# A LayerNorm, attention and ternary FFN kernel: both ends reordered, and two half-filled stationaries packed into one

## The chip, the cores and the metric

The kernel runs on one core of a Trainium2 chip. Its time is device microseconds from start to end of one execution; the figure for a kernel is the median of its runs. A core has a tensor engine (TensorE, in the profile PE, with weight loads as PEld), a vector engine (DVE), a scalar engine (ACT), GpSimd (POOL) and a synchronisation engine (SP). Each takes its instructions strictly in order and waits on semaphores for the others. DMAs are issued from the instruction streams of SP and ACT (in the profile SPq and ACTq). In this kernel TensorE multiplies a stationary of at most 128x128 by a moving operand of at most 512 columns and writes to PSUM, from which DVE and ACT read.

## The reference

The input x is 2048 x 256 (one batch, 32-bit floats). One layer normalisation feeds two branches, and both are added to x:

```python
xn = layernorm(x)                      # no scale, no offset
qkv = xn @ Wqkv.T                      # 16 heads of 128 for q, k and v
w = softmax(q @ k.T * 128 ** -0.5)     # 2048 x 2048 per head, no mask
attention = (w @ v) @ Wout.T           # 2048 -> 256
x1 = xn @ quantize(w1).T               # 256 -> 704
x2 = xn @ quantize(w2).T               # 256 -> 704
ffn = (sigmoid(x1) * x2) @ quantize(w3).T   # 704 -> 256
out = x + attention + ffn

def quantize(w):                       # weights -1, 0, 1
    gamma = mean(abs(w))
    return clip(round(w / (gamma + 1e-8)), -1, 1)
```

The inner width of the FFN, 704, is five times 128 and a rest of 64.

## The kernel before

**Sizes.** Rows are worked on in four chunks of 512 (NB = 4, QB = 512), each of four tiles of 128 (TB = 4). The key dimension has 16 tiles (NKT). Heads come in pairs (G = 2) whose weights are loaded together. The FFN's inner width has six chunks f (FC = 6); the last has only 64 columns. All orders are written out by hand: each engine does its instructions in the order in which the program makes them.

**The front (lines 320 to 344).** `loads` issues all early loads. Then one turn for each row chunk c: `turned` transposes the normalised chunk on PE (eight transposes, line 215, tile `pxn`), ACT copies it to `xnT` (line 216); `normalized` makes the next chunk on DVE; `magnitude` lets ACT sum the absolute values of one FFN matrix (tile `abs`); `q_piece(0, c)` and `v_piece(0, 2 * c)` make q of head 0 and one of eight v pieces of the first pair; `magnitude_of_all` sums over partitions by a matmul with ones (tile `pg`). After the four turns `quantize` makes the three ternary matrices on DVE (`w0q`, `w1q`, `w2q`: one comparison into `low`, one into the result), and `k_piece(0, c)` makes k of head 0. `halved` splits a value into a high part (ACT cast to the f32r type) and a low part (DVE): products with exact ternary weights are made from both parts.

**The FFN loop (lines 345 to 354).** 24 steps (c, f). `hidden` makes both first products of a step, w1's into one bank of a PSUM tile `ph` and w2's into the other: four matmuls each (line 275; 64 stationary columns where f is 5). ACT takes the sigmoid, DVE multiplies, `halved` splits. `summed` runs two steps later and adds the step's part of the second product into two PSUM tiles `pf` (line 297); after f = 5 ACT copies them to `yT`. `added` transposes `yT` back (line 314, tile `pyt`) and DVE adds it to y (line 317). The last `summed` and `added` run inside the attention's first steps.

**PSUM and small banks.** There are three two-bank tiles of the tag s (scores, `ph`, `pxn`, `pyt`), one bank m and one bank av. Before the attention's steady part, `bank` deals m and av out in turn to q, k and v pieces; ACT's copy of a piece frees its bank.

**Attention (lines 453 to 522).** Block n is one head and one row chunk, 64 in all; step v is one row tile, 256 in all. `scores(v)` makes two score tiles (line 374), DVE takes maxima (line 379), ACT exponentials (line 388). `exchanged(v)` moves the 128 x 2048 block of exponentials between partition groups by 16 DMAs of 64 KB, ten from SP and six from ACT (line 398); `transposed(v)` finishes the transposition on DVE in 32x32 squares (line 415) into `pT`. `weighted(n, k)` multiplies v by `pT` (line 421, tile `av`), ACT copies the result to `oT` (line 428), `projected(n, u)` multiplies by the output weights (line 439, tile `po`), and DVE scales by the inverse sums and adds into y (line 445). Scores run six steps ahead (LEAD) of `weighted`; in these first six steps, fillers from the table `first` stand between scores:

```python
1: [("v", 0, 1), ("v", 0, 3)], 2: [("v", 0, 5), ("v", 0, 7)],
3: [("k", 1, 0), ("k", 1, 1)], 4: [("k", 1, 2), ("q", 1, 0)], 5: [("k", 1, 3), ("q", 1, 1)],
```

In the steady part, k and q pieces of the next head and one v piece of the next pair per block are spread over the steps. A row chunk's result goes out by one DMA of 512 KB (line 450).

Of the kernel before, what the change touches and what calls it, by code (L numbers as in the profile page):

```python
# [19 lines left out]
def layernorm_attention_bitffn_kernel(  # L20
# [14 lines left out]
    nc = tc.nc  # L35
# [110 lines left out]
    def loads(fraw):  # L146
# [17 lines left out]
        for i, (src, cols) in enumerate(((w1T, FF), (w2T, FF))):  # L164
            w = fraw.tile([P, KC, FF], F32, tag=f"w{i}", name=f"w{i}s")
            nc.sync.dma_start(w, src.rearrange("(c p) f -> p c f", p=P))
            raw.append(w)
# [3 lines left out]
        if rest:  # L171
            nc.gpsimd.memset(w[:, whole, :], 0.0)
# [3 lines left out]
        if rest:  # L176
            nc.sync.dma_start(w[:rest, whole, :], w3T[whole * P :, :])
# [39 lines left out]

    ones = fw.tile([P, P], F32, tag="ones", name="ones")
# [16 lines left out]
    def quantize(fraw, i: int, w):  # L235

        wf = w.rearrange("p c f -> p (c f)")

        pos = fraw.tile([P, 1], F32, tag=f"pos{i}", name=f"pos{i}")
        neg = fraw.tile([P, 1], F32, tag=f"neg{i}", name=f"neg{i}")  # L240
        nc.vector.tensor_scalar(
            pos, pgs[0][:, 0, i : i + 1], 0.5 / (FF * DM), 0.5 * Q_EPS, ALU.mult, ALU.add
        )
        nc.vector.tensor_scalar(neg, pos, -1.0, None, ALU.mult)
        low = fraw.tile([P, FC * DM], F32, tag="low", name=f"low{i}")
        lo = low[:, : wf.shape[1]]
        wq = fw.tile(list(w.shape), F32R, tag=f"w{i}q", name=f"w{i}q")
        nc.vector.tensor_scalar(lo, wf, neg, None, ALU.is_lt)
        nc.vector.scalar_tensor_tensor(
            wq.rearrange("p c f -> p (c f)"), wf, pos, lo, ALU.is_gt, ALU.subtract  # L250
        )
        quantized[i] = wq
# [3 lines left out]

    xs, hids, yTs = {}, {}, {}

# [10 lines left out]
    def hidden(fp, c: int, f: int):  # L269
        m = min(P, FF - f * P)  # L270
        ph = ps_s.tile([P, 2, QB], F32, tag="s", name=f"ph{c}_{f}")
        todo = [(d, i) for i in (1, 0) for d in range(KC)]
        for j in range(2):
            for d, i in todo:
                nc.tensor.matmul(  # L275
                    ph[:m, j, :], quantized[j][:, d, f * P : f * P + m], xs[c][i][:, d],
                    start=((d, i) == todo[0]), stop=((d, i) == todo[-1]),
                )
        sg = fp.tile([P, QB], F32, tag="sg", name=f"sg{c}_{f}", bufs=2)
        nc.scalar.activation(sg[:m], ph[:m, 0, :], AF.Sigmoid)  # L280
        nc.vector.tensor_tensor(sg[:m], sg[:m], ph[:m, 1, :], ALU.mult)
        hid = [fp.tile([P, QB], F32R, tag=f"hid{i}", name=f"hid{i}{c}_{f}", bufs=4) for i in "hl"]
        halved(hid[0][:m], hid[1][:m], sg[:m])
        hids[c, f] = hid

    def summed(fp, c: int, f: int):

        m = min(P, FF - f * P)
# [6 lines left out]
        for e in range(DM // P):  # L295
            for i in (1, 0):
                nc.tensor.matmul(  # L297
                    yTs[c][e], quantized[2][:m, f, bass.ts(e, P)], hid[i][:m],
# [8 lines left out]
    def added(c: int):  # L307

        yT = yTs.pop(c)
        pt = ps_s.tile([P, 2, QB], F32, tag="s", name=f"pyt{c}")  # L310
        ptv = pt.rearrange("p a (b e) -> p (a b) e", e=DM)
        for t in range(TB):
            for e in range(DM // P):
                nc.tensor.transpose(  # L314
                    ptv[:, t, bass.ts(e, P)], yT[:, e, bass.ts(t, P)], ident
                )
        nc.vector.tensor_tensor(ys[c], ptv, ys[c], ALU.add)  # L317


    with tc.manual_schedule():  # L320
# [5 lines left out]
        with tc.tile_pool(name="fraw", bufs=1) as fraw:  # L326
            raw = loads(fraw)
            xns = {0: normalized(fraw, 0)}
            for c in range(NB):
                turned(xns.pop(c), c)  # L330
                if c + 1 < NB:
                    xns[c + 1] = normalized(fraw, c + 1)
                if c:
                    magnitude(fraw, c - 1, raw[c - 1])
                q_piece(0, c)
# [3 lines left out]
            for i, w in enumerate(raw):  # L339
                quantize(fraw, i, w)  # L340
                if i == 0:
                    halved_x(0)
        for c in range(NB):
# [3 lines left out]
        for i, (c, f) in enumerate(chunks):  # L347
# [3 lines left out]
            if i > 1:  # L351
# [65 lines left out]
    def weighted(n: int, k: int):  # L417
        h, b = blocks[n]
        if k == 0:
            avs[n] = ps_av.tile([P, QB], F32, tag="av", name=f"av{n}")  # L420
        nc.tensor.matmul(  # L421
            avs[n], vs[h // G, k // 2][:, k % 2, bass.ts(h % G, D)],
            pTs[n].rearrange("p t g (k q) -> p (t g) k q", q=32)[:, :, k, :],
            start=(k == 0), stop=(k == NKT - 1),
        )
        if k == NKT - 1:
            oT = apool.tile([P, QB], F32, tag="oT", name=f"oT{n}", bufs=1)
            nc.scalar.copy(oT, avs.pop(n))  # L428
            oTs[n] = oT

    def projected(n: int, u: int):

        h, b = blocks[n]
        if n == NBK - 1 and u % 2:
            pm = ps_s.tile([P, 2, QB], F32, tag="s", name=f"po{n}_{u}")[:, :, :DM]
        else:
            pm = ps_m.tile([P, 2, DM], F32, tag="m", name=f"po{n}_{u}")
        for j in range(2):
            nc.tensor.matmul(  # L439
                pm[:, j, :], oTs[n][:, bass.ts(2 * u + j, P)], weights[h // G, "o"][:, h % G, :],  # L440
# [8 lines left out]
        if u == TB // 2 - 1 and h == H - 1:  # L449
            nc.sync.dma_start(  # L450
                out[b * QB : (b + 1) * QB, :].rearrange("(t p) d -> p t d", p=P), ys[b]
            )
# [5 lines left out]
        1: [("v", 0, 1), ("v", 0, 3)], 2: [("v", 0, 5), ("v", 0, 7)],  # L458
        3: [("k", 1, 0), ("k", 1, 1)], 4: [("k", 1, 2), ("q", 1, 0)], 5: [("k", 1, 3), ("q", 1, 1)],
# [3 lines left out]
    with tc.manual_schedule():  # L463

        nc.scalar.activation(warm, ident[:, 0:1], AF.Exp)
        for u in range(-LEAD, NBK * TB):
# [7 lines left out]
            if lead_in:  # L474
# [9 lines left out]
                elif v == 3 and H > G:  # L484
                    load_weights(1, "v")
            elif t == 0:
                if n // GB + 1 < H // G:
                    v_piece(n // GB + 1, n % GB)
# [30 lines left out]
        inverses(NBK - 1)  # L519
        for u in range(TB // 2):  # L520
            projected(NBK - 1, u)
# [38 lines left out]
```

## Time and profile before

| What | us |
|---|---|
| median of three runs | 2309.71 (2309.66 to 2311.34) |
| profiled execution, its own time | 2309.66 |
| its span, first to last instruction | 2307.9 |
| PE busy | 2286.2 |
| DVE busy | 1463.5 |
| ACT busy | 771.8 |
| idle of PE that waits name | 16.3 |
| granted TensorE clock, mean | 0.998 |

In the page and the views, a group's name is line, engine, operation and tiles, written as out<-in with buffer numbers left out. A wait row reads: engine and line, what released it, us in total, times, longest. A busy PE is not PE at its peak: matmuls are pipelined, so that the start-to-start time of a run of matmuls says more than the length of one. A timeline row gives start, length, engine, line, operation, tiles, count, and in brackets the idle time before it and what ended it.

### The profile page before, as it was taken

How to read it: one execution, taken by the hardware profiler on the slowest of the kernel's cores; microseconds unless marked ns; L12 is line 12 of the kernel's file. 1: busy time of each engine (PE TensorE's matmuls, PEld its weight loads, DVE VectorE, ACT ScalarE, POOL GpSimd, SP SyncE). 2: the span in 40 equal slices, each digit the busy share in tenths (PEclk: the TensorE clock that was granted, in tenths of full speed). 3: DMA queues.
4: the chain of work that ended last, by engine and by line, in shares of the span. 5: the costliest groups of instructions: out<-in, count | busy, mean ns of one | idle time of the engine just before them, and what ended most of it. 6: DMA issues, size and time to landing. Idle time of an engine off the chain costs nothing.

```text
span 2307.9 us, 22750 instructions
## 1 busy us (share of the span) xinstructions
PE 2286.2 (99%) x6022; PEld 1136.2 (49%) x6022; DVE 1463.5 (63%) x1800; ACT 771.8 (33%) x1360; POOL 1.1 (0%) x8
## 2 busy tenths in 40 slices
PE   8999999999999999999999999999999999999997
PEld 6754444444444444444444444444444444444443
DVE  6566666666666666666666666566566666666774
ACT  5443333333333333323333333333333333333331
POOL 0000000000000000000000000000000000000000
PEclk9999999999999999999999999999999999999999
DMA  2055555555554555555555555555545555555554
GB/s 93 0 144 136 132 122 129 124 136 121 127 127 119 137 127 120 125 131 133 119 123 131 130 125 126 125 123 137 127 119 126 126 136 122 121 128 128 136 140 107
DMA packets 210977, 284.89 MB, mean 123 GB/s; under 512 B 66272, under 2 KB 79264, under 8 KB 210848
## 3 DMA queue, kind: packets, MB, share of 16 engines
q1 hardware_dynamic: 136448, 182.03, 32.6%
q10 hardware_dynamic: 74400, 101.42, 18.3%
q8 instruction: 47, 0.77, 0.2%
q14 instruction: 82, 0.67, 0.1%
HBM read 12.65 MB, written 2.10 MB: 6 GB/s over the span
## 4 chain that ended last, share of the span: by engine, by line
PE 97%; SPq 1%; DMA 0%; ACT 0%; DVE 0%; issue 0%; ACTq 0%; DVEq 0%
PE s L374 38%; PE av L421 37%; PE pq L116 5%; PE pv L132 5%; PE pk L106 5%; PE po L439 5%; PE ph L275 2%; PE pf L297 1%; SPq L398 1%; DMA part<-p 0%; PE pxn L215 0%; ACT xnT L216 0%; ACT p L388 0%; PE pyt L314 0%; DMA y<-in_x_dram 0%
## 5 line engine op out<-in xcount | busy, mean ns | idle before, releaser
L379 DVE TENSOR_REDUCE mx<-s 128x1 f32<-128x1024 f32 x512 | 627.0, 1225 | 706.8 <-PE s L374 706.8
L388 ACT ACTIVATE p<-s,nm 128x1024 f32<-128x1024 f32 x512 | 566.1, 1110 | 1394.8 <-DVE nm L382 627.1
L421 PE MATMUL av<-pT,v 128*128 128x512 f32 x2048 | 922.1, 593 | 6.3 <-DVE ri L405 6.3
L374 PE MATMUL s<-kT,qT 128*128 128x512 f32 x2048 | 921.1, 592 | 1.4 <-DVE y L317 1.3
L415 DVE STREAM_TRANSPOSE pT<-part 128x1024 f32<-128x1024 f32 x512 | 606.4, 1223 | 22.3 <-DMA part<-p 11.2
L374 PEld LDWEIGHTS s<-kT,qT 128*128 128x128 f32 x2048 | 388.9, 190 | 464.4 <-issue 440.2
L421 PEld LDWEIGHTS av<-pT,v 128*128 128x128 f32 x2048 | 389.7, 190 | 445.9 <-issue 439.6
L445 DVE SCALAR_TENSOR_TENSOR y<-po,ri,y 128x256 f32<-128x256 f32 x256 | 112.0, 479 | 31.8 <-PE po L439 17.2
L439 PE MATMUL po<-wo,oT 128*128 128x256 f32 x512 | 131.3, 379 | 0.7 <-ACT oT L428 0.7
L439 PEld LDWEIGHTS po<-wo,oT 128*128 128x128 f32 x512 | 97.2, 190 | 68.5 <-issue 60.3
L116 PE MATMUL pq<-xnT,wq 128*128 128x512 f32 x256 | 120.7, 594 | 4.4 <-ACT xnT L216 4.4
L132 PE MATMUL pv<-wv,xnT 128*128 128x256 f32 x512 | 120.6, 379 | 0.0
L106 PE MATMUL pk<-xnT,wk 128*128 128x512 f32 x256 | 119.7, 592 | 0.0
L132 PEld LDWEIGHTS pv<-wv,xnT 128*128 128x128 f32 x512 | 97.3, 190 | 39.7 <-issue 29.2
L388 ACT ACTIVATION_READ_ACCUMULATOR p<-s,nm 128x1 f32 x512 | 100.3, 196 | 0.0
L116 PEld LDWEIGHTS pq<-xnT,wq 128*128 128x128 f32 x256 | 48.3, 190 | 64.7 <-issue 59.3
L106 PEld LDWEIGHTS pk<-xnT,wk 128*128 128x128 f32 x256 | 48.6, 190 | 60.7 <-issue 60.7
L428 ACT COPY oT<-av 128x512 f32<-128x512 f32 x64 | 37.5, 586 | 75.5 <-PE av L421 75.5
L382 DVE TENSOR_REDUCE nm<-mx 128x1 f32<-128x2 f32 x256 | 39.7, 155 | 28.2 <-DVE mx L379 1.4
L121 ACT ACTIVATE qT<-pq 128x512 f32<-128x512 f32 x64 | 38.1, 595 | 1.8 <-PE pq L116 1.8
L137 ACT COPY v<-pv 128x512 f32<-128x512 f32 x64 | 37.1, 583 | 4.5 <-PE pv L132 4.5
L110 ACT COPY kT<-pk 128x512 f32<-128x512 f32 x64 | 37.2, 583 | 3.8 <-PE pk L106 3.8
(67 smaller groups left out, 330.6 us busy)
## 6 DMA issues: line engine op xcount, KB each, us to landing
part<-p SPq DMA_DIRECT2D x2560, 64.0 KB, 2.0
part<-p ACTq DMA_DIRECT2D x1536, 64.0 KB, 2.1
wq<-in_wqkvT_dram SPq DMA_DIRECT2D x8, 256.0 KB, 2.9
wv<-in_wqkvT_dram SPq DMA_DIRECT2D x8, 256.0 KB, 2.9
wk<-in_wqkvT_dram SPq DMA_DIRECT2D x8, 256.0 KB, 2.9
wo<-in_woutT_dram SPq DMA_DIRECT2D x8, 256.0 KB, 2.8
out_dram<-y SPq DMA_DIRECT2D x4, 512.0 KB, 3.0
y<-in_x_dram SPq DMA_DIRECT2D x2, 512.0 KB, 7.9
```

What stands on the lines that cost most here:

```text
L106: nc.tensor.matmul(pm, w[:, d, bass.ts(h % G, D)], xnT_k[:, d, c], start=(d == 0), stop=(d == KC - 1),)
L116: nc.tensor.matmul(pm, w[:, d, bass.ts(h % G, D)], xnT[:, d, bass.ts(c, QB)], start=(d == 0), stop=(d == KC - 1),)
L132: nc.tensor.matmul(pm[:, j, :], xnT[:, d, bass.ts(2 * i + j, P)], w[:, d, :], start=(d == 0), stop=(d == KC - 1),)
L275: nc.tensor.matmul(ph[:m, j, :], quantized[j][:, d, f * P : f * P + m], xs[c][i][:, d], start=((d, i) == todo[0]), stop=((d, i) == todo[-1]),)
L374: nc.tensor.matmul(s[:, bass.ts(j, QB)], qTs[h, b][:, bass.ts(t, P)], kTs[h][:, i * HALF + j * QB : i * HALF + (j + 1) * QB], start=True, ...
L379: nc.vector.tensor_reduce(mx[:, i : i + 1], s, AX.X, ALU.max)
L382: nc.vector.tensor_reduce(nm, mx, AX.X, ALU.max, negate=True)
L388: nc.scalar.activation(p, s, AF.Exp, bias=nm, accum_out=sums[n][:, t, i : i + 1],)
L415: nc.vector.transpose(pTs[n][:, t, g : g + 2], part[:, g : g + 2])
L421: nc.tensor.matmul(avs[n], vs[h // G, k // 2][:, k % 2, bass.ts(h % G, D)], pTs[n].rearrange("p t g (k q) -> p (t g) k q", q=32)[:, :, k, ...
L439: nc.tensor.matmul(pm[:, j, :], oTs[n][:, bass.ts(2 * u + j, P)], weights[h // G, "o"][:, h % G, :], start=True, stop=True,)
L445: nc.vector.scalar_tensor_tensor(ys[b][:, t, :], pm[:, j, :], rinvs[n][:, t : t + 1], ys[b][:, t, :], ALU.mult, ALU.add,)
```

## The change

- Front: `quantize` of the first two matrices moves into the turns 2 and 3. Turns 1, 2 and 3 get one more v piece (1, 3, 5), ahead of the q piece. `halved_x(0)` stands ahead of the last `quantize`. Two of the four k pieces of head 0 move between the first steps of the FFN loop.
- Last FFN chunk: the last 64 columns of both first matrices are quantized into one stationary `wlast` of 128 columns. `hidden` makes one product for f = 5: the first matrix's results lie on partitions 0 to 63, the second's on 64 to 127. ACT's sigmoid goes from the lower to the upper partitions, and all that follows, the last rows of w3 too, stands on partitions 64 to 127.
- Hand-over: the last `added` uses two tiles from `bank`, of four transposes each, and not a tile s; DVE adds in two halves. The table `first` holds the last v piece, head 1's pieces, and three v pieces of the second pair, which blocks 0 to 2 no longer make; the second pair's v weights are loaded at step 1, not 3.
- Tail: the last block's `weighted` and `projected` leave the loop. The columns of block 63 are made in two halves, the second in a tile s, with the projections of block 62 and of the first half between them. The last head's results go out by two tiles in a DMA, those of the last block by one tile, the last of each pair from ACT.

```diff
-            nc.gpsimd.memset(w[:, whole, :], 0.0)
+            nc.gpsimd.memset(w[:LAST, whole, :], 0.0)
...
-            nc.sync.dma_start(w[:rest, whole, :], w3T[whole * P :, :])
+            nc.sync.dma_start(w[LAST:, whole, :], w3T[whole * P :, :])
...
+    LAST = P - FF % P
...
-        wq = fw.tile(list(w.shape), F32R, tag=f"w{i}q", name=f"w{i}q")
...
-        nc.vector.scalar_tensor_tensor(
-            wq.rearrange("p c f -> p (c f)"), wf, pos, lo, ALU.is_gt, ALU.subtract
-        )
+        lo = lo.rearrange("p (c f) -> p c f", c=w.shape[1])
+        if i == 0:
+            quantized["last"] = fw.tile([P, KC, P], F32R, tag="wlast", name="wlast")
+        whole = FF // P * P if i < 2 else w.shape[2]
+        wq = fw.tile([P, w.shape[1], whole], F32R, tag=f"w{i}q", name=f"w{i}q")
+        parts = [(wq, 0, whole)]
+        if i < 2:
+            parts.append((quantized["last"][:, :, i * LAST : (i + 1) * LAST], whole, FF))
+        for o, f0, f1 in parts:
+            nc.vector.scalar_tensor_tensor(
+                o, w[:, :, f0:f1], pos, lo[:, :, f0:f1], ALU.is_gt, ALU.subtract
+            )
...
     def hidden(fp, c: int, f: int):
-        m = min(P, FF - f * P)
...
-        for j in range(2):
+        if f == FC - 1:
+            ws = [quantized["last"]]
+        else:
+            ws = [quantized[j][:, :, bass.ts(f, P)] for j in range(2)]
+        for j, w in enumerate(ws):
             for d, i in todo:
                 nc.tensor.matmul(
-                    ph[:m, j, :], quantized[j][:, d, f * P : f * P + m], xs[c][i][:, d],
+                    ph[:, j, :], w[:, d], xs[c][i][:, d],
...
+        p0 = LAST if f == FC - 1 else 0
...
-        nc.scalar.activation(sg[:m], ph[:m, 0, :], AF.Sigmoid)
-        nc.vector.tensor_tensor(sg[:m], sg[:m], ph[:m, 1, :], ALU.mult)
+        nc.scalar.activation(sg[p0:], ph[: P - p0, 0, :], AF.Sigmoid)
+        nc.vector.tensor_tensor(sg[p0:], sg[p0:], ph[p0:, len(ws) - 1, :], ALU.mult)
...
-                    yTs[c][e], quantized[2][:m, f, bass.ts(e, P)], hid[i][:m],
+                    yTs[c][e], quantized[2][p0:, f, bass.ts(e, P)], hid[i][p0:],
...
     def added(c: int):
...
+        if c < NB - 1:
+            pt = ps_s.tile([P, 2, QB], F32, tag="s", name=f"pyt{c}")
+            pts = [pt.rearrange("p a (b e) -> p (a b) e", e=DM)]
+        else:
+            pts = [bank([P, 2, DM], f"pyt{c}_{u}") for u in range(2)]
...
+            y = ys[c][:, u * m : (u + 1) * m]
+            nc.vector.tensor_tensor(y, pt, y, ALU.add)
...
+                if c > 1:
+                    quantize(fraw, c - 2, raw[c - 2])
                 if c:
                     magnitude(fraw, c - 1, raw[c - 1])
+                if c:
+                    v_piece(0, 2 * c - 1)
                 q_piece(0, c)
...
-            for i, w in enumerate(raw):
-                quantize(fraw, i, w)
-                if i == 0:
-                    halved_x(0)
-        for c in range(NB):
+            halved_x(0)
+            quantize(fraw, len(raw) - 1, raw[-1])
+        for c in range(2):
             k_piece(0, c)
...
-            if i > 1:
+            if i < 2:
+                k_piece(0, i + 2)
+            else:
                 summed(fp, *chunks[i - 2])
...
-    def weighted(n: int, k: int):
+    def weighted(n: int, k: int, part=None):
+
         h, b = blocks[n]
+        t0, t1 = (0, TB) if part is None else (part * TB // 2, (part + 1) * TB // 2)
         if k == 0:
-            avs[n] = ps_av.tile([P, QB], F32, tag="av", name=f"av{n}")
+            pool, tag = (ps_s, "s") if part else (ps_av, "av")
+            avs[n] = pool.tile([P, QB], F32, tag=tag, name=f"av{n}_{t0}")
...
-        if u == TB // 2 - 1 and h == H - 1:
-            nc.sync.dma_start(
-                out[b * QB : (b + 1) * QB, :].rearrange("(t p) d -> p t d", p=P), ys[b]
-            )
+
+            if h == H - 1 and (j or n == NBK - 1):
+                t0 = t if n == NBK - 1 else t - 1
+                (nc.scalar if n == NBK - 1 and j else nc.sync).dma_start(
...
-        1: [("v", 0, 1), ("v", 0, 3)], 2: [("v", 0, 5), ("v", 0, 7)],
-        3: [("k", 1, 0), ("k", 1, 1)], 4: [("k", 1, 2), ("q", 1, 0)], 5: [("k", 1, 3), ("q", 1, 1)],
+        1: [("v", 0, NV - 1), ("k", 1, 0)], 2: [("k", 1, 1), ("k", 1, 2)],
+        3: [("k", 1, 3), ("q", 1, 0)], 4: [("q", 1, 1), ("v", 1, 0)], 5: [("v", 1, 1), ("v", 1, 2)],
...
-        for u in range(-LEAD, NBK * TB):
+        for u in range(-LEAD, (NBK - 1) * TB):
...
-                elif v == 3 and H > G:
                     load_weights(1, "v")
             elif t == 0:
-                if n // GB + 1 < H // G:
-                    v_piece(n // GB + 1, n % GB)
+                g = n // GB + 1
+                if g < H // G and ("v", g, n % GB) not in made:
+                    v_piece(g, n % GB)
...
-        inverses(NBK - 1)
-        for u in range(TB // 2):
-            projected(NBK - 1, u)
+
+        n = NBK - 1
+        for i in range(n - 1, n + 1):
+            inverses(i)
+        for k in range(NKT):
+            weighted(n, k, 0)
+            if k in (KQ - 1, 3 * KQ - 1):
+                projected(n - 1, k // (2 * KQ))
+        for k in range(NKT):
+            weighted(n, k, 1)
+            if k == KQ - 1:
+                projected(n, 0)
+        projected(n, 1)
```

## The prediction

> **What bounds the kernel now.** First the page's busy shares: TensorE (PE) has work 99% of the span, and its chain row gives PE 97%. So the end moves by what PE no longer does, and by the holes in its work. The list of PE's waits names every hole:
>
> ```profile
> PE 2286.2 (99%) x6022; PEld 1136.2 (49%) x6022; DVE 1463.5 (63%) x1800; ACT 771.8 (33%) x1360; POOL 1.1 (0%) x8
> ```
> ```profile
> PE av L421 <- DVE ri L405: 6.3, 1, 6.3
> PE pq L116 <- ACT xnT L216: 4.4, 4, 1.1
> PE pf L297 <- issue: 2.2, 1, 2.2
> ...
> PE s L374 <- DVE y L317: 1.3, 1, 1.3
> PE po L439 <- ACT oT L428: 0.7, 1, 0.7
> ```
>
> All lie within 126 us of the start or 32 us of the end; between, PE issues without a hole. The stage windows (columns: stretch; its length, then busy us and count by engine; PEclk is the granted clock) show what two holes cost besides: after 2.2 and 6.3 us idle the clock is granted at 0.63 and 0.71, near half for some 3.5 us.
>
> ```profile
> 47.40:51.60 4.20, 4.20 (x14) 3.34 (x13) 3.24 (x5) 2.66 (x4) 0.00 (x0) 0.63 0.00 0
> ...
> 126.00:2276.30 2150.30, 2150.30 (x5488) 1042.34 (x5486) 1384.17 (x1644) 708.16 (x1261) 0.00 (x0) 1.00 0.54 129
> 2276.30:2287.90 11.60, 5.32 (x9) 2.27 (x9) 2.59 (x4) 0.59 (x1) 0.00 (x0) 0.71 0.27 77
> ```
>
> Two more timelines (start, length, engine, line) carry the sum: ScalarE (ACT) at the hand-over from FFN to attention, where its copies of v stand behind two exponentials and six DMA issues; and the last 32 us.
>
> ```profile
> 119.77 5.00 ACTq L398 DMA_DIRECT2D part<-p  x5
> 124.87 1.11 ACT L388 ACTIVATE p<-s,nm 128x1024 f32<-128x1024 f32 x1 [4.80 <-DMA part<-p]
> ...
> 127.06 0.58 ACT L137 COPY v<-pv 128x512 f32<-128x512 f32 x1
> ...
> 127.53 0.60 ACT L137 COPY v<-pv 128x512 f32<-128x512 f32 x1
> ```
> ```profile
> 2276.45 0.59 ACT L428 COPY oT<-av 128x512 f32<-128x512 f32 x1 [7.59 <-PE av L421]
> ...
> 2280.18 2.37 DVE L415 STREAM_TRANSPOSE pT<-part 128x1024 f32<-128x1024 f32 x2 [3.98 <-DMA part<-p]
> ...
> 2282.69 5.41 PE L421 MATMUL av<-pT,v 128*128 128x512 f32 x8 [6.28 <-DVE ri L405]
> ...
> 2300.86 1.99 PE L439 MATMUL po<-wo,oT 128*128 128x256 f32 x8 [0.73 <-ACT oT L428]
> 2302.03 1.74 DVE L445 SCALAR_TENSOR_TENSOR y<-po,ri,y 128x256 f32<-128x256 f32 x4 [7.57 <-PE po L439]
> ```
>
> Start-to-start prices, from the timeline: a 512-column f32 matmul is two instructions of 0.43 us, a 256-column one two of 0.215; an FFN product (f32r) is one of 0.23. So a q, k or v piece is 1.72 us and 32 `av` instructions are 13.7. Below, times are on the old trace's clock.
>
> **The front (0 to 51.6 us): 7.2 us gained.** Three v pieces (3 x 1.72 = 5.16 us) move from later work, which PE bounds, into the turns of the chunk loop, where PE waits 1.1 us for each `xnT` copy. Turn 1: transposes start at 13.95 and take 0.87; v1 to 16.57; q1 to 18.29. v2 needs the bank that v1's copy frees, and that copy stands on ACT behind `abs0` (17.98 + 0.19), so it ends near 18.7: a wait of 0.45. v2 to 20.46, `pg` to 20.75. Turns 2 and 3 are 0.87 + 3 x 1.72 + 0.3 = 6.3 each without a wait, by the same copying on ACT: 33.4, where the old kernel was at 31.49.
>
> VectorE (DVE): the first two quantizations (3.2 us each, with 0.15 to 0.3 for each added small piece) move into its idle stretches; `xl0`, behind v6's copy and the cast, is ready at 36.2, and the third quantization ends at 39.4. PE does k0, k1 to 36.9, so it doesn't wait for `xl0`. With k2, k3 between the first hidden chunks, hidden, k, hidden, k, hidden end at 45.8. The old first `pf` started 4.2 after the end of `w2q` (42.05 to 46.24); by the same chain it could start at 43.6, so the 2.2 us wait is gone, and with it the half-clock stretch. The next `pf`, hidden, `pf` take 3.65 and end at 49.5; the old kernel got there at 51.57. Gain 2.07 + 5.16 = 7.2. Bounds: 5 (a bank wait like 0.45 in every turn, a late `pf`) to 7.7 (no wait at all).
>
> **Last FFN chunk: 3.7 us gained.** The eight 64-column products of a chunk lasted 54.29 to 56.13, as long as eight of 128 columns. Four go, four times: 16 x 0.23 = 3.7. What follows them on ACT and DVE keeps its count and length (64 partitions took 0.59 and 0.68 against 0.60 and 0.69), and `summed` still comes two chunks later: 3.7 us (1.83 + 0.91 + 0.92) beside a chain of 3.0. Products from the upper 64 rows stand in no row; those from the lower 64 cost some 0.2 more per chunk at the change of shape (four in 1.12 against 0.91). I take the same; bounds -0.8 to +1.2 in all.
>
> **Hand-over: 4.7 us lost.** The 1.3 us wait of `s` for the add of y goes: the last transposes (`pyt`) now use the two small banks. But these were just filled by v7 and the first k piece of head 1, and they come free by ACT's copies. PE is through with both at 123.3; the copies, second and third after `p1`, end at 127.64 and 128.13 by the rows above. So `pyt`'s first half waits 4.4 us, the second ends at 128.65, and behind it in PE's order stand the scores of step 2, which started at 125.69: 3.0 lost. DVE's maxima and ACT's exponentials of step 2 only follow. Bounds of this: 1.2, if ACT's five issues took 5 x 0.63 and not 5.00 (the DMA view of 118 to 125 us has an instruction fetch in it, which may fall elsewhere), to 3.5. The clock comes on top: 2.2 us idle was enough for a half-clock stretch at 47, 1.3 us was not at 125. I take 3.4 us at half, 1.7 lost; bounds 0 to 2.6.
>
> [...]
>
> **Steady part: nothing.** Blocks 0 to 2 lose their v piece (counted above). The second v weights are loaded two steps earlier, ahead of two steps' exchanges on SP's queue: 0.6 us of issue there, while the exchange's transposes ended 2.7 us before PE needed them at this pace (last head: 2254.6 against 2257.4).
>
> **The tail: 7.0 us gained.** PE's last `av` of block 62 leaves its place at 2276.27; block 63's first half needs only `pT` rows that were ready at 2269.9, and the bank that `oT`'s copy frees at 2277.04. So: 2277.1; 8 x 0.215, `po` 0.86, 16 x 0.215 to 2283.1. The second `po` of block 62 needs the y update of the first, which on DVE stands behind the last transposes (2282.55), two more reciprocals' pairs (0.7) and 0.9 of updates: 2284.2, a wait of 1.1. Behind it: 0.86, then 8 x 0.215 to 2286.8, the second half with `po` of block 63 (6.9 + 0.86) to 2294.6. Copy of half a tile 0.37 (0.59 for 512 columns, 1.01 for 1024), `po` at 2295.05; updates at +1.17 (as 2300.86 to 2302.03), 0.88 long: 2297.1. The last DMA is 128 KB, and loads of that size landed after 2.5 to 2.7: 2299.8; after the old landing the span went on 1.15: 2300.9 against 2307.9. SP's extra output issues ahead of exchanges cost 0.4 us each (0.37 to 0.53 in the rows), but those exchanges waited for ACT's DMAs anyway; bounds of the tail 5 (the last exchange 1 us later, a short fall of the clock) to 8.
>
> **Sum.** 7.2 + 3.7 - 4.7 + 7.0 = 13.2. The profiled execution took 2309.66 by its own time (span 2307.9 and 1.8 around it); the median shown is 2309.71. 2309.7 - 13.2 = 2296.5.
>
> **Rivals.**
> 1. *As above*, 2296.5: 0.53.
> 2. *The hand-over's wait is short*: 1.2 lost and no fall of the clock. For it: the fetch that stretched ACT's issues. Against: PE's stream is only 16 instructions ahead there (12 v products at four each, less 16 FFN products at two). 2309.7 - (7.2 + 3.7 - 1.2 + 7.0) = 2293.0: 0.22.
> 3. *The ends give less*: front 5, FFN 2.5, tail 5, hand-over 4.7: 2301.9. For it: ACT's and DVE's strict order in the front. Against: slack of 2.2 us at `pf`. 0.18.
> 4. *No difference*: a second fall of the clock in the tail and 6 us lost at the hand-over beside rival 3, above 2305.1: 0.04.
> 5. *Slower*: without their v piece, blocks 0 to 2 run at SP's pace, ten issues of 0.63 a step. One step of 6.87 us lost at the start of each of three blocks is 20.6: 2317.1. It decides from 18 us on. Against: the last head runs at this pace and PE has no wait in it. 0.03.
>
> Under 0.2% (4.6 us) a measurement of this kernel can't tell from no change. Faster 0.93, same 0.04, slower 0.03. The range reaches from rival 2 with its other bounds, 2291, to rival 3, 2302.
>
> **What would show it.** In the profile after: no `pf` wait and clock 1.00 near 47 us; four products in the last chunk; a new PE wait of `pyt` for ACT's copy of v, 2.5 to 4.5 us, and a low clock after it; no 6.3 us wait of `av`, one near 1 us of `po` for y; about 4 us from the last update to the end. Wrong it would be if ACT copies before its DMA issues, if a copy holds PE in each turn, or if the exchange falls behind in blocks 0 to 2.

## The result, and the profile after

The changed kernel takes 2293.84 us (median of six runs, 2292.64 to 2295.35); the old one, in runs beside it, 2309.74 (2307.87 to 2311.34). The ratio is 0.9931, with a 95% interval of 0.9919 to 0.9944. That is 15.9 us faster; 2296.5 was forecast, with a range of 2291 to 2302. The profiled execution took 2294.3 by its own time, with a span of 2292.5 against 2307.9: 15.4 less. The stages below are compared by the two profiled executions.

The page's line of busy time, and then all waits of PE over 0.2 us in the changed kernel:

```profile
PE 2280.0 (99%) x6038; PEld 1139.0 (50%) x6038; DVE 1464.0 (64%) x1803; ACT 771.1 (34%) x1361; POOL 1.1 (0%) x8
```
```profile
PE pyt L336 <- ACT v L137: 2.5, 1, 2.5
PE idle L348 <- POOL ident masks.py:199: 1.5, 1, 1.5
PE po L468 <- DVE y L474: 1.2, 1, 1.2
PE pq L116 <- ACT xnT L216: 1.1, 1, 1.1
PE pxn L215 <- DVE xn L205: 0.8, 1, 0.8
PE av L452 <- ACT oT L459: 0.7, 1, 0.7
PE po L468 <- ACT oT L459: 0.5, 1, 0.5
PE pv L132 <- ACT v L137: 0.3, 1, 0.3
```

The 6.3 us wait of `av`, the 2.2 us wait of `pf` and three of four waits of `pq` are gone. The new one is the first: the last y transposes wait 2.5 us for ACT's copy of a v piece. The stage windows (stretch; its length, then busy us and count of PE, PEld, DVE, ACT and POOL; granted clock; DMA) show what it costs besides:

```profile
47.40:51.60 4.20, 4.20 (x20) 3.50 (x19) 2.61 (x4) 2.79 (x5) 0.00 (x0) 1.00 0.01 4
117.66:121.07 3.41, 0.96 (x9) 0.88 (x9) 0.25 (x1) 2.90 (x6) 0.00 (x0) 1.00 0.61 159
121.07:124.48 3.41, 3.41 (x6) 1.40 (x5) 1.04 (x2) 0.00 (x0) 0.00 (x0) 0.50 0.80 218
126.24:2268.30 2142.06, 2142.02 (x5461) 1037.21 (x5459) 1383.03 (x1643) 703.97 (x1254) 0.00 (x0) 1.00 0.54 129
2268.30:2292.50 24.20, 18.07 (x80) 14.95 (x80) 6.21 (x14) 1.33 (x3) 0.00 (x0) 0.99 0.23 71
```

Around 47 us the clock is whole now. From 121.07, after a stretch of 3.41 us in which PE worked only 0.96, it is granted at half for 3.41 us. That isn't so in every execution: half a clock for 3.41 us leaves a mean of 0.9993, and two of the six runs, the fastest (2292.64 and 2293.17), have a mean granted clock of 1.000: in these it can't have been at half for such a stretch anywhere. The long stretch has no hole (2142.02 busy of 2142.06) and is 5.17 shorter than its counterpart in the old kernel (2147.23 from the first filler of step 2 to the same copy of `oT`): three v pieces of 1.72.

ACT at the hand-over (timeline: start, length, engine, line):

```profile
112.98 0.61 ACTq L425 DMA_DIRECT2D part<-p  x1
113.62 3.57 ACTq L425 DMA_DIRECT2D part<-p  x5
117.30 1.11 ACT L415 ACTIVATE p<-s,nm 128x1024 f32<-128x1024 f32 x1 [3.39 <-DMA part<-p]
...
119.49 0.58 ACT L137 COPY v<-pv 128x512 f32<-128x512 f32 x1
```

The order is the forecast one: five issues, two exponentials, then the copy that PE waits for. But the five issues take 3.57 and not 5.00. The tail, from the last `oT` copy of block 62:

```profile
2268.30 0.59 ACT L459 COPY oT<-av 128x512 f32<-128x512 f32 x1 [7.84 <-PE av L452]
...
2272.79 2.37 DVE L442 STREAM_TRANSPOSE pT<-part 128x1024 f32<-128x1024 f32 x2 [4.78 <-DMA part<-p]
...
2276.49 1.13 PE L468 MATMUL po<-wo,oT 128*128 128x256 f32 x4 [1.25 <-DVE y L474]
...
2287.64 1.13 PE L468 MATMUL po<-wo,oT 128*128 128x256 f32 x4 [0.52 <-ACT oT L459]
2288.81 0.88 DVE L474 SCALAR_TENSOR_TENSOR y<-po,ri,y 128x256 f32<-128x256 f32 x2 [5.95 <-PE po L468]
```

While the exchange and DVE finish the last rows of `pT`, PE makes the first half of block 63's columns; the end comes 2.8 us after the last update, where the prediction had expected about 4. By stages, with each stage's own start taken out:

| Stage | before | after | gained |
|---|---|---|---|
| start to the scores of step 1 | 115.95 | 109.80 | 6.15 |
| from there to the first filler of step 2 | 13.27 | 16.44 | -3.17 |
| from there to the last `oT` copy of block 62 | 2147.23 | 2142.06 | 5.17 |
| from there to the end | 31.41 | 24.22 | 7.19 |

The sum is 15.34, the difference of the two spans 15.35.

### The profile page after: what moved, and what is told of

Its sections match the earlier page's. It is cut to its first block, busy times and chain, and to the rows that moved or that the text cites. A ratio compares the mean times of both kernels' runs of the same rounds, so it can differ in the third digit from the quotient of the medians.

```text
span 2292.5 us, 22790 instructions
## 1 busy us (share of the span) xinstructions
PE 2280.0 (99%) x6038; PEld 1139.0 (50%) x6038; DVE 1464.0 (64%) x1803; ACT 771.1 (34%) x1361; POOL 1.1 (0%) x8
## 4 chain that ended last, share of the span: by engine, by line
PE 97%; SPq 1%; DVE 1%; DMA 0%; ACT 0%; issue 0%; DVEq 0%; ACTq 0%
PE s L401 38%; PE av L452 37%; PE po L468 5%; PE pk L106 5%; PE pq L116 5%; PE pv L132 5%; PE ph L291 2%; SPq L425 1%; PE pf L314 1%; DMA part<-p 0%; PE pyt L336 0%; PE pxn L215 0%; DMA y<-in_x_dram 0%; ACT p L415 0%; DVE mx L406 0%
## 5 line engine op out<-in xcount | busy, mean ns | idle before, releaser
L452 PE MATMUL av<-pT,v 128*128 128x512 f32 (+1 forms) x2080 | 920.7, 586 | 0.7 <-ACT oT L459 0.7
L452 PEld LDWEIGHTS av<-pT,v 128*128 128x128 f32 x2080 | 395.1, 190 | 435.8 <-issue 426.7
L132 PEld LDWEIGHTS pv<-wv,xnT 128*128 128x128 f32 x512 | 96.9, 190 | 39.7 <-issue 26.8
L459 ACT COPY oT<-av 128x512 f32<-128x512 f32 (+1 forms) x65 | 37.6, 579 | 71.7 <-PE av L452 71.7
```

Of the source, the lines that this page charges most:

```text
L132: nc.tensor.matmul(pm[:, j, :], xnT[:, d, bass.ts(2 * i + j, P)], w[:, d, :], start=(d == 0), stop=(d == KC - 1),)
L452: nc.tensor.matmul(av, vs[h // G, k // 2][:, k % 2, bass.ts(h % G, D)], pTs[n][:, t0:t1].rearrange("p t g (k q) -> p (t g) k q", q=32)[:, ...
```

## Experiments

### What the wait at the hand-over comes from: three runs

The first is the changed kernel again. In the second, PE's warm-up is changed without changing its length:

```diff
-        for i in range(32):
+        wide = ident.unsqueeze(1).to_broadcast([P, QB // P, P])
+        for i in range(16):
             nc.tensor.transpose(idle[:, i % 2, :P], ident, ident)
+        for i in range(2):
+            nc.tensor.matmul(
+                idle[:, i].rearrange("p (b q) -> p b q", q=P), ident, wide, start=True, stop=True
+            )
```

and in the third 16 transposes are added where PE waits:

```diff
-        for i in range(32):
+        for i in range(39):
             nc.tensor.transpose(idle[:, i % 2, :P], ident, ident)
...
                 turned(xns.pop(c), c)
+                if c == 0:
+                    for i in range(9):
+                        nc.tensor.transpose(idle[:, i % 2, :P], ident, ident)
```

Expected of the first:

> The changed kernel itself, beside which the three others are read: 2293.8 us as before, with PE's wait of pyt for a copy of v at 2.5 us and 3.4 us of half clock from about 121 us. If these two move by more than 0.3 us from one execution to the next, the hand-over is no fixed cost and the other runs can't be read from it.

Expected of the second:

> Of the 32 warm-up transposes the last 16 (1.8 us) give way to two 512-column products of the same length in all, so that PE's stream is 12 instructions shorter and nothing else moves. Theory 1 (the instruction fetch stretches DMA issues): the 16 KB fetch that fell at 113.0 falls 2 to 3 us later, within ScalarE's five DMA issues of the first step; these take about 5.0 us and not 3.57, the wait of pyt grows from 2.5 to about 3.9, and the time to 2295.2. Rival (the pace of those issues comes from what they move, not from the fetch): 3.6 and 2.5 us as before, 2293.8, wherever the fetch is.

Expected of the third:

> The changed kernel with 16 more warm-up transposes, put where TensorE waits anyway (seven ahead of the first transposes, nine in the wait for the first copy of xnT), so that its stream is 16 instructions longer before the hand-over. Theory (the fetch of instructions stretches the DMA issues that it meets): it falls 2 to 3 us earlier against the first scores of step 1, before ScalarE's five issues; these take 5 x 0.63 = 3.2 us, and the wait of pyt falls to 2.1, the lower bound of the prediction's reasoning. Rival (the issues are slow because of one another): 3.6 to 4.2 and 2.5 to 3.0 us as in the two profiles of the changed kernel.

Measured: 2294.19 us, 2295.66 and 2293.58 (five, five and four runs; the third on another chip, where the old kernel took 2309.93 and not 2309.59). ACT's five issues (timeline) and PE's wait (list of waits) in the changed kernel again:

```profile
113.31 4.16 ACTq L425 DMA_DIRECT2D part<-p  x5
```
```profile
PE pyt L336 <- ACT v L137: 3.0, 1, 3.0
```

in the kernel with the shorter stream:

```profile
113.55 4.35 ACTq L430 DMA_DIRECT2D part<-p  x5
```
```profile
PE pyt L336 <- ACT v L137: 3.2, 1, 3.2
```

and in the kernel with the longer stream:

```profile
113.65 3.17 ACTq L428 DMA_DIRECT2D part<-p  x5
```
```profile
PE po L471 <- DVE y L477: 2.1, 1, 2.1
PE pyt L336 <- ACT v L137: 2.0, 1, 2.0
```

In the DMA records the queue q8, whose packets are of the kind "instruction", has one packet of 16 KB near here. The DMA view of 2 us finds it at 112.5 to 114.5 in the changed kernel, at 114.5 to 116.5 with the shorter stream and at 104 to 106 with the longer one (queue, kind: packets, MB, share of 16 engines' time; 3.4% of 16 times 2 us is 1.09 us):

```profile
q8 instruction: 1, 0.02, 3.4%
```
```profile
q8 instruction: 1, 0.02, 4.0%
```
```profile
q8 instruction: 1, 0.02, 3.0%
```

It starts at 112.96 in the changed kernel's first profile (and lasts 1.08 us), at 112.68 in its second (1.57), at 114.93 with the shorter stream (1.27), and at 104.24 with the longer one, before any of these DMAs is issued. The longest of ACT's five issues, made while the packet is moved, lasts 0.73, 1.30 and 1.52 us in the first three, and SP's 1.23, 1.80 and 1.24; in the fourth no issue of ACT's step takes over 0.61, and the five take 3.17. They take 3.17 in the kernel with the front alone too (below), whose packet comes at 107.01, 10 us ahead of them. So the fetch is the cause of the stretch, as the theory has it, and without it the wait is 2.0. In all four profiles the wait of `pyt` is the length of the five issues less some 1.1 us.

Three things were forecast wrongly. The first run shows that the hand-over is no fixed cost: the same kernel had 2.5 and 3.0 us, with 0.5 us of difference in how long the packet took. Moving the fetch behind ACT's first issues, where the old kernel has it, gave 3.2 us of wait, not 3.9; the packet took 1.27 us here and 1.73 in the old kernel. And with the longer stream the fetch moved by 8.8 us against the scores of step 1 for 16 instructions, not by the 2 to 3 expected (with the shorter one, by 2.0 for 12, as expected); what sets its place stays open.

Of the 2.6 us that the second run's span is above the first's, only 0.2 lie at the hand-over. 2.1 lie in the tail, where `po` waited 1.9 us for y and the clock fell:

```profile
2275.77:2279.18 3.41, 1.53 (x7) 1.21 (x7) 2.12 (x8) 0.00 (x0) 0.00 (x0) 1.00 0.13 45
2279.18:2282.59 3.41, 3.41 (x10) 2.71 (x9) 0.71 (x2) 0.37 (x1) 0.00 (x0) 0.50 0.33 108
```

The same happened in the profile of the third (wait 2.1, tail 26.8 us against 24.2 to 24.6 where the clock stayed whole). So the totals of these two runs say less than their hand-overs.

### What the two small banks cost at the hand-over

One run puts the last y transposes back into a tile s:

```diff
-        if c < NB - 1:
-            pt = ps_s.tile([P, 2, QB], F32, tag="s", name=f"pyt{c}")
-            pts = [pt.rearrange("p a (b e) -> p (a b) e", e=DM)]
-        else:
-            pts = [bank([P, 2, DM], f"pyt{c}_{u}") for u in range(2)]
+        pt = ps_s.tile([P, 2, QB], F32, tag="s", name=f"pyt{c}")
...
+        nc.vector.tensor_tensor(ys[c], ptv, ys[c], ALU.add)
```

The other keeps the banks and makes the transposes ahead of the fillers of step 1:

```diff
             if lead_in:
+                if v == 1:
+                    added(NB - 1)
                 for what, hg, i in first.get(v, ()):
...
                 elif v == 1:
-                    added(NB - 1)
                     front.close()
```

Expected of the tile s:

> The last y transposes go back into one tile of the tag s, as in the old kernel; all else is the new kernel's. Theory 1 (the two small banks are what costs): nothing on PE waits for the copies of v7 and k. Scores of step 2 then need the exponential of the first half of step 1, which ends at 118.4, and start there instead of at 121.13: 2.7 us. No gap is long enough for a fall of the clock: 1.6 us more. 2293.8 - 4.3 = 2289.5. Rival: ScalarE's chain of exponentials and DMA issues holds the lead-in whatever PE does, and the wait only turns up at the third step's bank: less than 1 us of gain, 2293.0.

Expected of the transposes first:

> The two small banks stay, but the y transposes stand ahead of v7 and the first k piece of head 1, when the copies of pf have long freed both banks. Theory 1: v7 waits for DVE's first add (after the maxima of step 1, which end at 115.34: add to 116.0), k for the second; PE idles 1.0 and 0 us where it idled 2.5, v7 ends at 117.7, k at 119.4, where step 2 starts instead of at 121.13, at full clock. 1.7 + 1.6 = 3.3 gained: 2290.5. Rival, as for the run with one tile s: less than 1 us, 2293.0.

Measured: 2291.74 us (2291.34 to 2291.85) and 2291.11 (2291.03 to 2291.32), against 2294.19 (2292.99 to 2294.99) for the changed kernel on the same chip. The waits at this place, with the tile s:

```profile
PE s L395 <- DVE y L334: 1.3, 1, 1.3
```

and with the transposes first, with the window of step 2's scores below it:

```profile
PE pv L132 <- DVE y L340: 0.9, 1, 0.9
```
```profile
119.29:122.72 3.43, 3.43 (x9) 1.52 (x8) 1.23 (x1) 1.52 (x4) 0.00 (x0) 1.00 0.68 200
```

From the scores of step 1 to the first filler of step 2 it is 13.61 and 13.18 us, against 17.02 in the changed kernel beside them and 13.27 in the old one. The hand-over's loss is thus shown to come from using the small banks right after v7 and the k piece have filled them: without that, 3.4 to 3.8 us less by the traces and 2.5 and 3.1 by the medians. The rival (ScalarE holds the lead-in anyway) is out. With the tile s, less came than forecast: step 2 starts at 119.77 and not at 118.5, for it waits for DVE's add of y, which ends at 119.7. That is the old 1.3 us wait: the old kernel's row, `PE s L374 <- DVE y L317`, was right, and the expectation, which put the exponential in its place, was not.

### The parts by themselves

Three kernels are the old one with one part each: the front, with the fillers' table that goes with it (its core below),

```diff
+                if c > 1:
+                    quantize(fraw, c - 2, raw[c - 2])
                 if c:
                     magnitude(fraw, c - 1, raw[c - 1])
+                if c:
+                    v_piece(0, 2 * c - 1)
...
-        1: [("v", 0, 1), ("v", 0, 3)], 2: [("v", 0, 5), ("v", 0, 7)],
+        1: [("v", 0, NV - 1), ("k", 1, 0)], 2: [("k", 1, 1), ("k", 1, 2)],
```

the packed stationary,

```diff
-        for j in range(2):
+        if f == FC - 1:
+            ws = [quantized["last"]]
+        else:
+            ws = [quantized[j][:, :, bass.ts(f, P)] for j in range(2)]
+        for j, w in enumerate(ws):
```

and the tail:

```diff
-        for u in range(-LEAD, NBK * TB):
+        for u in range(-LEAD, (NBK - 1) * TB):
...
+        for k in range(NKT):
+            weighted(n, k, 0)
+            if k in (KQ - 1, 3 * KQ - 1):
+                projected(n - 1, k // (2 * KQ))
```

Expected of the front alone:

> The old kernel with the front alone: early quantization, the three moved v pieces, two k pieces between the first FFN steps, and the table of fillers that goes with them. By the prediction's steps 7.2 us of gain (5.16 for three v pieces that the steady part no longer makes, 2.07 at the first pf) and no loss at the hand-over, where the y transposes keep their tile s: 2309.6 - 7.2 = 2302.4. Rival (the moved v pieces are paid for in the front, a bank wait of 0.45 in each turn, or blocks 0 to 2 fall behind their exchanges): 5 us or less, 2304.6 or more.

Expected of the packed stationary alone:

> The old kernel with the packed stationary alone. Theory: 16 products of 0.23 us go, 3.7 us, and the first scores start 3.7 us earlier: 2305.9. Rival (another shape or the upper 64 rows cost what is saved, or the chain of sigmoid, product and split behind the products becomes the bound in the last chunks): a gain of 2.5 us or less, 2307.1.

Expected of the tail alone:

> The old kernel with the new tail alone: two halves of the last block with the projections between them, and small output DMAs. By the prediction's sum 7.0 us, by the traces of both kernels 7.25: 2302.4. Rival (the front's gain shifts the last exchanges, so that part of these 7.25 came from there): 5 us, 2304.6.

Measured, against 2309.45 us for the old kernel beside them (21 runs): 2303.26 (gain 6.2; ratio 0.9973, interval 0.9962 to 0.9983), 2306.10 (3.4; 0.9985, 0.9976 to 0.9994) and 2303.09 (6.4; 0.9972, 0.9962 to 0.9982). The medians lie nearer to the three theories than to their rivals, though each kernel is 0.2 to 0.9 us slower than expected. The intervals alone don't rule the rivals out (that of the packed stationary reaches from 1.4 to 5.5 us, and its rival was 2.5; for the front and the tail, from 4 to 9 us, it was 5). The traces below do: 5.5 to 6.95, 3.4 and 7.17 us in the stages concerned.

Part of the reason can be read. The packed stationary alone and the tail alone keep the old front, and their waits of `pf` are the old ones:

```profile
PE pf L314 <- issue: 2.4, 1, 2.4
```
```profile
PE pf L297 <- issue: 2.2, 1, 2.2
```

but in neither did the clock fall, as it did in the old kernel's profiled execution. The windows around that wait, of the old kernel and of the tail alone:

```profile
43.64:47.05 3.41, 1.25 (x6) 0.72 (x6) 1.98 (x3) 1.80 (x4) 0.00 (x0) 1.00 0.00 0
47.05:50.47 3.42, 3.42 (x10) 2.68 (x9) 2.11 (x4) 2.41 (x4) 0.00 (x0) 0.50 0.00 0
```
```profile
42.66:46.07 3.41, 1.53 (x7) 0.94 (x5) 1.20 (x2) 2.60 (x4) 0.00 (x0) 1.00 0.00 0
46.07:49.48 3.41, 3.13 (x14) 2.61 (x15) 2.07 (x4) 1.74 (x4) 0.00 (x0) 1.00 0.00 0
```

With the clock whole, the old front's scores of step 1 start at 114.46 (the tail alone), not at 115.95. Against that the front alone, at 113.55, gains 0.9 there, and against the old kernel's profile 2.4. With 5.17 from the three v pieces, less 0.3 lost at the hand-over (13.60 us) and 0.3 in the old tail (31.70; its wait of `av` is 6.9 where it was 6.3), that makes 5.5 against an execution without that half clock and 6.95 against the one with it. The median's 6.2 lies between. The packed stationary alone, whose scores of step 1 start at 110.73, gains 3.73 there, which is the forecast 3.7, and loses 0.4 in the old tail (31.77): 3.4, as its median has it. The tail alone gains 7.17 in its stage; why its median shows only 6.4 isn't settled, but the profiled run, with a mean clock of 1.000, is the fastest of nine (2300.99 to 2305.10), and seven of the others have 0.999 or 0.998.

### The rest of the tail, and a faster kernel

The kernel with the transposes first also gets tiles s for the odd projections and for the first half of block 63's columns:

```diff
-            pool, tag = (ps_s, "s") if part else (ps_av, "av")
+            pool, tag = (ps_s, "s") if part == 0 else (ps_av, "av")
...
-        pm = ps_m.tile([P, 2, DM], F32, tag="m", name=f"po{n}_{u}")
+        if n >= NBK - 2 and u % 2:
+            pm = ps_s.tile([P, 2, QB], F32, tag="s", name=f"po{n}_{u}")[:, :, :DM]
+        else:
+            pm = ps_m.tile([P, 2, DM], F32, tag="m", name=f"po{n}_{u}")
```

> The new kernel with the y transposes ahead of the fillers, and in the tail with tiles s for the odd projections and for the first half of the last block's columns. Theory: the wait of po for y (1.2 to 1.9 us in the traces so far) and the wait of av for oT (0.7) go, beside what the y transposes' place gave (3.1): 2294.2 - 3.1 - 1.9 = 2289.2. Rival (VectorE's last transposes and updates, not PE's banks, set the end of the tail): the waits turn up as a wait of the second half for its pT rows, and the time is that of the kernel with the y transposes first, 2291.1.

Measured: 2288.27 us (2288.25 to 2289.66), ratio 0.9909 to the old kernel, interval 0.9895 to 0.9922. All that is left of PE's waits over 0.2 us:

```profile
PE idle L348 <- POOL ident masks.py:199: 1.5, 1, 1.5
PE pq L116 <- ACT xnT L216: 1.1, 1, 1.1
PE pv L132 <- DVE y L340: 0.9, 1, 0.9
PE po L471 <- ACT oT L459: 0.5, 1, 0.5
PE pxn L215 <- DVE xn L205: 0.4, 1, 0.4
PE pv L132 <- ACT v L137: 0.3, 1, 0.3
```

Both waits of the tail are gone and none took their place; the stage takes 21.8 us instead of 24.5. This kernel is 5.6 us faster than the changed one by medians (2288.27 against 2293.84), 5.1 by their ratios to the old kernel, and the fastest of the study.

On it, the last row chunks' results go out in one DMA each, as in the old kernel:

```diff
-            if h == H - 1 and (j or n == NBK - 1):
-                t0 = t if n == NBK - 1 else t - 1
...
+        if u == TB // 2 - 1 and h == H - 1:
+            nc.sync.dma_start(
+                out[b * QB : (b + 1) * QB, :].rearrange("(t p) d -> p t d", p=P), ys[b]
+            )
```

Expected of the same kernel once more, and of this one:

> The kernel with both cures once more, beside which the next one is read: 2288.3 us.

> The kernel with both cures, but each row chunk's result goes out in one DMA of 512 KB as in the old kernel. Theory (the landing depends on the size): from the last update's end to the end of the span it was 4.1 us in the old kernel with 512 KB and 2.8 with 128 KB; the time grows by about 1.3, to 2289.6, so that of the tail's 7.25 us some 6 come from the order of the work. Rival (the landing is a fixed delay, and the old 4.1 us came from something else): 2288.5.

Measured: 2288.59 us (2288.42 to 2288.74) and 2289.64 (2289.44 to 2289.73). The last update in each (spans 2286.9 and 2287.9):

```profile
2283.20 0.88 DVE L477 SCALAR_TENSOR_TENSOR y<-po,ri,y 128x256 f32<-128x256 f32 x2 [5.95 <-PE po L471]
```
```profile
2283.09 0.88 DVE L477 SCALAR_TENSOR_TENSOR y<-po,ri,y 128x256 f32<-128x256 f32 x2 [5.95 <-PE po L471]
```

From its end to the end of the span it is 2.85 and 3.89 us. So about 1.0 us of the tail's 7.2 came from the smaller output DMAs (1.3 by the traces of the old and the changed kernel, 4.09 and 2.83) and some 6 from the order of the work. The run changes the issuing engine with the size, ACT to SP; at the same size ACT's DMAs don't land sooner (64 KB of `part` in the old kernel: 2.1 us from ACT, 2.0 from SP), so that the size is the likelier cause.

### When the clock falls

> The kernel with both cures and, behind its last projection, a probe that belongs to no result: three series of ten rounds, in each of which TensorE makes 5, 8 or 13 transposes and waits about 1.2 us for a 1024-column copy on ScalarE; 64 transposes without a wait stand ahead of each series. Rounds of 0.55, 0.87 and 1.42 us of work make idle shares of about 68%, 58% and 46%, with no gap over 1.3 us. Theory 1 (the share of idle time in a window of 3.41 us decides, and some 55% is enough): the clock falls to half in the first two series and stays whole in the third. Theory 2 (one long gap is wanted, 1.9 us or more): no fall in any series. The time grows by some 75 us.

The probe, behind the last projection:

```diff
+        for busy in (5, 8, 13):
+            for i in range(64):
+                nc.tensor.transpose(probe[:, i // 4 % 2, bass.ts(i % 4, P)], ident, ident)
+            for r in range(10):
+                gone = ppool.tile([P, HALF], F32, tag="p", name=f"gone{busy}_{r}", bufs=4)
+                nc.scalar.copy(gone, probe.rearrange("p a q -> p (a q)"))
+                for i in range(busy):
+                    nc.tensor.transpose(probe[:, i // 4 % 2, bass.ts(i % 4, P)], ident, ident)
```

Measured in one execution, by windows of the probe: the 3.41 us ahead of the first series' half-clock stretch and the stretch itself, then the same of the second, the 64 dense transposes behind it with the third's first round, and the third:

```profile
2289.98:2293.39 3.41, 1.20 (x10) 0.92 (x10) 0.00 (x0) 2.02 (x2) 0.00 (x0) 1.00 0.00 0
2293.39:2317.28 23.89, 14.74 (x62) 11.55 (x61) 0.00 (x0) 8.10 (x8) 0.00 (x0) 0.50 0.00 1
...
2327.52:2330.93 3.41, 1.57 (x12) 1.34 (x13) 0.00 (x0) 1.64 (x2) 0.00 (x0) 1.00 0.00 0
2330.93:2354.82 23.89, 16.95 (x75) 14.55 (x73) 0.00 (x0) 6.07 (x6) 0.00 (x0) 0.50 0.00 1
2354.82:2363.00 8.18, 6.62 (x58) 6.14 (x57) 0.00 (x0) 1.33 (x2) 0.00 (x0) 1.00 0.00 0
2363.00:2388.00 25.00, 14.74 (x117) 12.61 (x117) 0.00 (x0) 8.79 (x9) 0.00 (x0) 1.00 0.00 1
```

No wait of PE was longer than 1.2 us, and the clock fell in the first two series and not in the third. So theory 2 falls: here it wasn't one long gap that decided. The stretches at half clock that lie behind a hole and end within the execution lasted 3.41 us (one in the old kernel, from 47.05, one in the changed one), 6.83 (the old kernel, from 2279.37) and 23.89 (the probe, twice): one, two and seven times 3.41. The two of the old kernel start 2232.32 us apart, 654 steps of 3.4133, and so lie on one grid. What went with the fall was how much of one step of that grid PE idled, counted by the trace's modelled ends of the products. The clock fell after steps with 2.95 and 2.16 us of idle time (old kernel, from 2275.96 and from 43.64), 2.45 (changed kernel), 2.21 and 1.84 (probe) and 1.88 (tail with the shorter stream). It did not fall after 1.88 (new tail alone), 1.55 (packed stationary alone) and 1.25 (tail of the changed kernel), nor in the probe's third series, where rounds of 2.80 us with holes of 1.16 leave at most 1.77 in a step. That puts the border near 1.85 us in these runs, about 55% of a step. In the probe, the steps that brought the two falls had their idle time in gaps of at most 1.2. Once at half, the clock stayed there for a second step in the old kernel, where the first (from 2279.37) had 3.32 us of idle time, and was whole after steps with none (from 47.05 and from 2282.79); the probe's two stretches of seven steps held 9.15 and 6.94 us of it. The time grew by 102 us and not by 75; the rounds lasted 1.9 to 2.8 us at full clock and up to 3.1 at half.

## Why the prediction was right, and which term was off

- **What bounds the kernel**, and so that the end moves by PE's work and holes: shown. The long stretch changed by the moved work alone (5.17 against 5.16 forecast), and the kernels that end a wait of PE end earlier by at least that wait.
- **Front, 7.2.** Right by steps: the first `pf` started at 45.78 (45.8 forecast), the hidden chunk behind the second at 49.42 (49.5), k at 33.27 (33.4), and the bank wait in turn 1 was 0.27 (0.45). Of what came at `pf` (2.07 forecast, some 2.4 measured), though, 1.5 was the old profile's half-clock stretch, which two other profiles of the same front didn't have. Without it the front gives 0.9 there, beside the 5.2 of the v pieces: against such an execution the forecast is too high by 1.1.
- **Last FFN chunk, 3.7.** Right: four products in 0.90 (52.14 to 53.04) instead of eight in 1.84, and 3.73 in the kernel that has this part alone. The upper 64 rows cost what the lower ones do (four products in 1.12, 58.58 to 59.70).
- **Hand-over, -4.7: the term that was mis-sized.** Its mechanism was right: the banks just filled, ACT's order, the scores of step 2 behind `pyt`, and, in most executions, the fall of the clock. But the wait was given as 4.4, from issues of 5.00, and measured 2.5 and 3.0, from issues of 3.57 and 4.16. Of the 1.9 us between 4.4 and 2.5, 1.4 are the issues; the other 0.5 is on PE's side, where the wait began 7.9 us after the scores of step 1 did (117.67 and 109.80) and not 7.35 (123.3 and 115.95). The 3.0 of loss by waiting were 1.6 and 2.6; the 1.7 of clock were 1.6 and 1.2. Together 3.2 and 3.7. The instruction fetch, which the prediction had seen as the lower bound's reason, decides between 2.0 and 3.2 us of wait; the old kernel's trace, from which the value was taken, has its longest packet (1.73).
- **The fall of the clock**, taken from the row at 47 us: right for the profiled executions, not for all. The clock fell in all four profiles that have this wait, of 2.0 to 3.2 us (in the changed kernel's first it put 2.45 us of idle time into one step); but by its mean, 1.000, it did not fall in two of the six runs of the result, nor in the fastest runs of the first experiment's three kernels (2292.99; 2294.92; 2292.39 and 2292.68). That fits the border near 1.85 us: where a step of the grid ends within a hole of 2.5 us, neither part need reach it.
- **Steady part, nothing:** shown; no wait in it, so that the rival in which blocks 0 to 2 run at SP's pace never came near.
- **Tail, 7.0.** 7.2 measured, with waits of 1.2 (1.1), 0.7 and 0.5 at the forecast places. That the sum agrees so well is partly luck. From the copy of `oT` to the end of the last update it took 21.4 us and not 20.65 (DVE's last transposes alone came 0.8 later after that copy than in the old kernel, 4.5 against 3.7); from the last update to the end it took 2.8 and not 3.8, where the prediction had added the old kernel's 1.15 to the landing time of a load. Its lower bound's "short fall of the clock" was real: the wait of `po` for y measured 1.2 to 2.1 us in seven profiles, and in two of them the clock fell and the tail took 2 us more.

So 13.2 forecast against 15.3 by the traces: 1.5 from the hand-over, 0.4 from front and FFN, 0.2 from the tail. The time lies nearer to the second rival's 2293.0 than to the likeliest case's 2296.5. Of that rival's two reasons, the fetch that stretched ACT's issues was half right (it fell elsewhere, but still within them), and no fall of the clock holds for two of the six runs, not for the profiled one: there the hand-over came out at 3.2, between its 1.2 and the likeliest case's 4.7. Rival 3, smaller gains at the ends, and the two rivals without a gain found no support in any stage.

## What to carry to other kernels

Before a tile is moved to another buffer to end one engine's wait, ask who filled that buffer last and where the copy that frees it stands in its engine's order; here a 1.3 us wait was exchanged for 2.5 to 3.0 and, in most executions, a clock at half. A duration that is read off one trace may hold a passing event such as an instruction fetch; look for rows of the same work without it, and take the value between. And a hole in TensorE's work was dearer here than its length where it brought the idle time in one step of 3.41 us above some 1.85: in the probe, two holes of 1.1 us (2.21 in a step) did it as well as one of 2.2 (2.16) did in the old kernel.

## What the runs showed of the hardware

- The fetch of 16 KB of instructions held up DMA issues on both queues at the hand-over: ACT's five issues of 64 KB took 3.17 us without it and 3.57 to 4.35 with it (5.00 in the old kernel); a single issue of 0.60 became 0.73 (changed kernel) to 2.14 (old kernel) on ACT's queue, one of 0.59 1.23 to 1.85 on SP's.
- The fall of the clock went with the idle time in a step of 3.41 us and not with the length of a gap: it came after the steps given above with 1.84 us or more, save one of the two with 1.88, and after none with 1.77 or less. Gaps of at most 1.2 us that made up 2.21 and 1.84 us of a step brought the clock to half, each time for seven steps.
- Whether a hole of 2 to 2.5 us cost some 1.5 us more (1.5 at `pf`, 1.6 and 1.2 at the hand-over) thus depended on where it fell on the grid, which differed from execution to execution: the wait of 2.2 us at `pf` put 2.16 us of idle time into one step of the old kernel (the clock fell) and 1.88 into one of the kernel with the new tail (it didn't). The changed kernel's times spread over 2.7 us, those of the kernel without such holes over 1.4 and 0.3 in its two sets of runs.
- With a last output DMA of 128 KB from ACT the execution ended 2.85 us after the last update, with one of 512 KB from SP 3.89.
